# Ranks inside each expert by differences on the matrix engine, and products that nobody reads in its pauses

## The chip, the cores and the metric

The kernel runs on one core of a Trainium2 chip. The metric is the device time of one execution in microseconds (us), lower is better. About 0.2%, or 3.2 us here, is what a measurement of this kernel can tell from no change.

A core has five engines that each work through their own queue in order: TensorE (PE, with its weight loads shown as PEld), VectorE (DVE), ScalarE (ACT), GpSimd (POOL) and SyncE (SP, which only issues DMAs here). They wait for each other by semaphores. TensorE's clock is granted by the chip; the profile gives the share of full speed as PEclk.

## The reference, cut to what matters

Four layers follow each other over 2048 tokens of 256 channels, each a conditioning block and a feed-forward block added to `x`. The change lies in the last feed-forward block, where each of 16 experts takes the 160 tokens with the highest top-1 probability among those that chose it:

```python
    def _L3_ffn_ref(x, Wg, W1, b1, W2, b2):      # n = 16, bt = 2048
        cap = math.ceil(CAP_FACTOR * bt / n)     # 160
        logits = jnp.einsum('btd,dn->btn', x, Wg)
        probs = jax.nn.softmax(logits, axis=-1)
        top1_val = probs.max(axis=-1).reshape(bt)
        top1_idx = probs.argmax(axis=-1).reshape(bt)
        masked = jnp.where(top1_idx[None, :] == jnp.arange(n)[:, None], top1_val[None, :], -jnp.inf)
        vals, idx = jax.lax.top_k(masked, cap)
        valid = jnp.isfinite(vals)
        xe = x_flat[idx]
        h = jax.nn.gelu(jnp.einsum('ncd,ndh->nch', xe, W1) + b1[:, None, :])
        out = jnp.einsum('nch,nhd->ncd', h, W2) + b2[:, None, :]
        safe_idx = jnp.where(valid, idx, bt)
        y_flat = x_flat.at[safe_idx.reshape(-1)].set(out.reshape(-1, d), mode='drop')
```

## The kernel before, in words

**Where the change sits.** `Last` is the last feed-forward block. The 2048 tokens are 16 tiles `t` of 128 and four chunks `q` of 512. A token's place in its expert's list is its rank: how many tokens of the same expert have a higher probability (or the same and an earlier index). `Last.chunk(q)` makes a list of small steps for each chunk, and `Last.finish` runs them in an order written out by hand (`todo`), between the last additions of the conditioning block (`c.pair`, two tiles at a time, whose inputs `yt` come by DMA). The compiler's scheduler then sets the order within each engine.

**The steps of a chunk.** `logits` multiplies by the gate (PE, `l3f_pt`) and copies (ACT, `l3f_lt`). `top` transposes (PE, `l3f_pl`) and finds on DVE the chosen expert `f` and the top probability `val`, with one exponential on ACT. `rows` makes the one-hot `oh` and its running count `cum`, and spreads `f` and `val` of 512 tokens over all 128 partitions: eight PE transposes (`l3f_rb`) and two ACT copies into `HT` (`self.eb`, `self.vb`). `last` is `rows` followed by `keep`, which stores the residual. Then come `beats(t)`, one unit for each tile `t` up to the chunk's own last: 4, 8, 12 and 16 units for chunks 0 to 3, 40 in all.

**A unit before the change.** ACT squares four times the difference of the experts' numbers (`l3f_dq`). DVE compares the probabilities of 512 tokens (fewer on the diagonal) with those of the tile's 128, and asks that the comparison exceed `dq`, which is zero only for the same expert (`l3f_b`, L1822, with the row sums accumulated into `self.acc`). The 16 diagonal units need three more DVE instructions over 128x128 for ties (`l3f_tie`, L1813, L1816, L1817). PE sums `l3f_b` over its partitions with products one column wide (`l3f_cs`, L1829), and DVE subtracts those sums (L1836).

**After the units.** DVE adds up `self.acc` to `l3f_rank` (L1875) and compares the ranks with a row of numbers, half of the tiles at a time (`l3f_A`, L1879); 32 small products (`l3f_pi`, L1884) turn this into token lists, four more (`l3f_pj`, L1892) rearrange the tail, `numbers` makes indices of them, POOL gathers the tokens' rows by indirect DMA (L332), and `Last.run` works through 20 slots: transposes (`ps_cm`, L354), a product (`l3f_ph`, L1945, or `l3f_gh` for a group of four experts), GELU on ACT, a product (`l3f_po`), two additions on DVE, and an indirect DMA to the output (L1933).

PSUM is used through pools: tag `mm` has four buffers, `o` and `t` two each.

Of the kernel before, what the change touches and what calls it, by code (L numbers as in the profile page):

```python
# [86 lines left out]
def _consts(k):  # L87
    nc, cp = k.nc, k.cp
    k.ident = cp.tile([P, P], F32, name="ident")
    make_identity(nc, k.ident)  # L90
    k.ones = cp.tile([P, P], F32, name="ones")
    nc.vector.memset(k.ones, 1.0)

    k.before = cp.tile([P, P], F32, name="before")
    nc.gpsimd.affine_select(out=k.before, in_=k.ones, compare_op=ALU.is_ge, fill=0.0,
                            base=-1, pattern=[[1, P]], channel_multiplier=-1)
    k.after = cp.tile([P, P], F32, name="after")
    nc.gpsimd.affine_select(out=k.after, in_=k.ones, compare_op=ALU.is_ge, fill=0.0,
                            base=-1, pattern=[[-1, P]], channel_multiplier=1)

    k.hm = cp.tile([P, 8], F32, name="hm")
    nc.gpsimd.affine_select(out=k.hm, in_=k.ones[:, 0:8], compare_op=ALU.is_ge, fill=0.0,
                            base=0, pattern=[[-16, 8]], channel_multiplier=1)
    nc.gpsimd.affine_select(out=k.hm, in_=k.hm, compare_op=ALU.is_ge, fill=0.0,
                            base=15, pattern=[[16, 8]], channel_multiplier=-1)
    ii = k.zero.bitcast(I32)[:, 0:CAP]
    nc.gpsimd.iota(ii, pattern=[[1, CAP]], base=0, channel_multiplier=0)
    k.iota = cp.tile([P, CAP], F32, name="iota")
    nc.vector.tensor_copy(k.iota, ii)
    nc.vector.memset(k.zero[:, 0:D], 0.0)  # L110
    nc.vector.memset(k.zero[:, D:], NONE)
    it = cp.tile([P, NT], I32, name="it")
    nc.gpsimd.iota(it, pattern=[[P, NT]], base=0, channel_multiplier=1)
    k.tok = cp.tile([P, NT], F32, name="tok")
    nc.vector.tensor_copy(k.tok, it)
    k.tok2 = cp.tile([P, NT], F32, name="tok2")
    nc.vector.tensor_scalar_mul(k.tok2, k.tok, 2.0)
    k.one16 = cp.tile([P, 1], BF16, name="one16")
    nc.vector.memset(k.one16, 1.0)

    k.small = {}
    for n, c, f in (("L2_wr", 4, 8), ("L2_gw", 2, 8), ("L3_wr", 4, 8), ("L3_Wg", 2, 16)):
        t = k.small[n] = cp.tile([P, c, 32], F32, name="w_" + n)
        nc.gpsimd.memset(t, 0.0)
        nc.scalar.dma_start(t[:, :, 0:f], k.A[n].rearrange("(c p) f -> p c f", p=P))
    for n in ("L2_rb", "L3_rb"):
        t = k.small[n] = cp.tile([P, 8], F32, name="w_" + n)
        nc.scalar.dma_start(t, k.A[n].to_broadcast([P, 8]))
    t = k.small["L3_b1"] = cp.tile([P, 64], F32, name="w_b1")
    nc.scalar.dma_start(t, k.A["L3_b1"])  # L130

    k.cT = cp.tile([P, 2, 2], F32, name="cT")
    nc.sync.dma_start(k.cT, k.A["condT"].rearrange("(c p) b -> p c b", p=P))
# [216 lines left out]
def _channel_major(k, psum, rows):  # L350

    ps = psum.tile([P, 2, P], F32, name="ps_cm", tag="t", bufs=2)
    for c in range(2):
        k.nc.tensor.transpose(ps[:, c, :], rows[:, c * P:(c + 1) * P], k.ident)  # L354
    return ps
# [849 lines left out]

def _shared(k, pool, psum, X, tb, W1, W3, W2, nf, hook=None, mid=None):
# [30 lines left out]
def _back(k, psum, src, dst, t, ref=None):  # L1237
# [6 lines left out]
    k.nc.scalar.copy(dst[:, :, t * P:(t + 1) * P], ps)  # L1244

# [45 lines left out]
class Tokens:  # L1291
# [28 lines left out]
    def back(self, t, ref=None):  # L1320
        _back(self.k, self.psum, self.dst, self.dstT, t, ref)
        self.put = t + 1

# [11 lines left out]
    def pair(self):  # L1335
# [3 lines left out]
        for t in range(self.put, self.added):  # L1339
            self.back(t)  # L1340
# [337 lines left out]
class Last:  # L1678

    E, F = 16, 512

    def __init__(self, k):
# [8 lines left out]
        self.neg = rp.tile([P, NT], F32, name="l3f_neg")  # L1693
        self.cum = rp.tile([P, NT + 1, E], F32, name="l3f_cum")

        self.acc = rp.tile([P, NT, 10], F32, name="l3f_acc")
# [4 lines left out]

        self.vb, self.eb = k.HT[:, 0, :], k.HT[:, 1, :]
# [12 lines left out]
    def begin(self):  # L1715

        k, nc = self.k, self.k.nc
        nc.vector.memset(self.acc, 0.0)
        nc.vector.memset(self.cum[:, 0, :], 0.0)
# [3 lines left out]
        self.weights()  # L1723

# [4 lines left out]
    def chunk(self, q):  # L1729
# [41 lines left out]
        def rows(mul, mm):  # L1771
            nc.vector.tensor_scalar_mul(self.neg[:, ts], got["f"], -4.0)
            oh = self.oh[:, ts, :]
            nc.vector.tensor_tensor(oh, _bc(self.down, 1, [P, 4, E]), _bc(got["f"], 2, [P, 4, E]),
                                    ALU.is_equal)
            for t in range(4 * q, 4 * q + 4):
                nc.vector.tensor_add(self.cum[:, t + 1, :], self.cum[:, t, :], self.oh[:, t, :])
            for src, dst in ((got["f"], self.eb), (self.val[:, ts], self.vb)):
                ps = psum.tile([P, 4, P], F32, name="l3f_rb", tag="mm")
                for j in range(4):  # L1780
                    i = nc.tensor.transpose(ps[:, j, :], src[:, j:j + 1].to_broadcast([P, P]), k.ident)  # L1781
                    behind(i, mm)
                nc.scalar.copy(dst[:, cols], ps.rearrange("p j q -> p (j q)"))
            ps = psum.tile([P, 4, E], F32, name="l3f_pn", tag="mm")
            i = nc.tensor.matmul(ps.rearrange("p t e -> p (t e)"), k.ones,
                                 self.cum[:, ts, :].rearrange("p t e -> p (t e)"), start=True, stop=True)
            behind(i, mm)

            w = pool.tile([P, 4, E], F32, name="l3f_w")
            nc.vector.tensor_mul(w, ps, oh)  # L1790
# [4 lines left out]
        def beats(t):  # L1795

            def unit(mul, mm):
                lo = max(t * P, q * TB)
                own = t >= 4 * q
                dq = pool.tile([P, TB], F32, name="l3f_dq", tag="fa")  # L1800
                n = (q + 1) * TB - lo
                i = nc.scalar.activation(dq[:, 0:n], self.eb[:, lo:lo + n], AF.Square,  # L1802
                                         bias=self.neg[:, t:t + 1], scale=4.0)
                v1 = self.val[:, t:t + 1]

                first = t % 4 == 0
                if first:
                    got["cs"] = psum.tile([P, 4], F32, name="l3f_cs", tag="t", bufs=2)
                a = lo
                if own:  # L1810
                    a = lo + P
                    tie = pool.tile([P, P], F32, name="l3f_tie", tag="xsT", bufs=3)
                    i = nc.vector.scalar_tensor_tensor(tie, self.vb[:, lo:a], v1, k.after, ALU.is_equal,  # L1813
                                                       ALU.mult)
                    behind(i, mul)
                    i = nc.vector.scalar_tensor_tensor(tie, self.vb[:, lo:a], v1, tie, ALU.is_gt, ALU.add)  # L1816
                    i = nc.vector.scalar_tensor_tensor(tie, tie, 1.0, dq[:, 0:P], ALU.mult, ALU.is_gt,  # L1817
                                                       accum_out=self.acc[:, t, 4:5])
                n = (q + 1) * TB - a
                if n:  # L1820
                    w = pool.tile([P, TB], BF16, name="l3f_b", tag="xs", bufs=4)
                    i = nc.vector.scalar_tensor_tensor(w[:, 0:n], self.vb[:, a:a + n], v1,  # L1822
                                                       dq[:, a - lo:a - lo + n], ALU.is_gt, ALU.is_gt,
                                                       accum_out=self.acc[:, t, q:q + 1])
                    behind(i, mul)

                    for j in range(n // P):
                        m = (a + j * P) // P - 4 * q
                        nc.tensor.matmul(got["cs"][:, m:m + 1], w[:, j * P:(j + 1) * P], k.one16,  # L1829
                                         start=first, stop=t % 4 == (2 if own else 3),  # L1830
                                         skip_group_check=True)
                        first = False
                if t % 4 == 3:

                    lo = 1 if own else 0
                    nc.vector.tensor_scalar_mul(self.acc[:, 4 * q + lo:4 * q + 4, 6 + t // 4],  # L1836
                                                got["cs"][:, lo:4], -1.0)
# [14 lines left out]
    def finish(self, c):  # L1852
# [3 lines left out]
        for e in range(E):  # L1856
# [4 lines left out]
                p1[3:7], p3[0:1], p1[7:], p2[2:3], p3[1:2], p2[3:7], p3[2:3], p2[7:], p3[3:]]  # L1861
        for x in todo:
            if callable(x):
                x()
            else:
                for p in x:
                    p(None, None)
# [7 lines left out]
        nc.vector.tensor_reduce(rank, self.acc, AX.X, ALU.add)  # L1875
        ps = k.psum.tile([P, 2, 2, E], F32, name="l3f_pi", tag="t", bufs=2)
        for h in range(2):
# [3 lines left out]
            for j in range(8):  # L1881
                t = 8 * h + j
                for o, r in ((ps[:, 0], slice(0, P)), (ps[0:32, 1], slice(P, CAP))):
                    nc.tensor.matmul(o, A[:, j, r], self.ids[:, t], start=t == 0 and r.start == 0,  # L1884
                                     stop=t == NT - 1, skip_group_check=True)
# [5 lines left out]
        for g in range(4):  # L1891
            nc.tensor.matmul(pg[32 * g:32 * g + 32], k.ident[0:32, 0:32], more[:, :, g::4], start=True,  # L1892
                             stop=True, skip_group_check=True)
# [20 lines left out]
    def run(self):  # L1914
# [70 lines left out]
        for n, i in enumerate(order):  # L1985
            xT = pool.tile([P, 2, P], F32, name="xsT", bufs=3)
            nc.vector.tensor_copy(xT, _channel_major(k, psum, at[i]))
# [154 lines left out]
```

## Time and profile before

| | us |
|---|---|
| median of 3 runs | 1601.93 (1601.33 to 1602.55) |
| the profiled execution, its own time | 1612.81 |
| its span in the profile | 1611.1 |
| mean granted clock of TensorE | 0.953 |

The profiled execution took 10.9 us more than the median of the plain runs. Times in the profile count from the start of its span. The ranks are made between about 1449 and 1508 us of it, the slots of the last block between 1514 and 1600 us. A row of a group shows the line, the engine, what is written and read, the count, the busy time and the mean length of one, and then how long the engine stood idle just before and what released it.

### The profile page before, as it was taken

How to read it: one execution, taken by the hardware profiler on the slowest of the kernel's cores; microseconds unless marked ns; L12 is line 12 of the kernel's file. 1: busy time of each engine (PE TensorE's matmuls, PEld its weight loads, DVE VectorE, ACT ScalarE, POOL GpSimd, SP SyncE). 2: the span in 40 equal slices, each digit the busy share in tenths (PEclk: the TensorE clock that was granted, in tenths of full speed). 3: DMA queues.
4: the chain of work that ended last, by engine and by line, in shares of the span. 5: the costliest groups of instructions: out<-in, count | busy, mean ns of one | idle time of the engine just before them, and what ended most of it. 6: DMA issues, size and time to landing. Idle time of an engine off the chain costs nothing. (4 is left out here: it accounts for less than half of the span.)

```text
span 1611.1 us, 23661 instructions
## 1 busy us (share of the span) xinstructions
PE 1466.1 (91%) x8570; PEld 1021.6 (63%) x8570; DVE 491.7 (31%) x1654; ACT 313.1 (19%) x637; POOL 293.5 (18%) x306
## 2 busy tenths in 40 slices
PE   5879998967999989999999999999999989995697
PEld 2543333533555776555599999999985448863575
DVE  3732221323411344341111111111114414459432
ACT  2312221112111212111111111111112212126322
POOL 0400000300231332023100000000000243430242
PEclk9879999977999999999999999999999999995699
DMA  9759994813211465051143255055517437573271
GB/s 241 262 181 334 343 345 161 246 54 118 83 50 40 148 210 178 27 194 49 40 172 104 101 184 169 30 181 178 175 32 259 149 118 243 186 224 124 59 242 35
DMA packets 184241, 252.46 MB, mean 157 GB/s; under 512 B 17111, under 2 KB 137823, under 8 KB 184112
## 3 DMA queue, kind: packets, MB, share of 16 engines
q1 hardware_dynamic: 164448, 210.92, 40.8%
q0 software_dynamic: 14176, 36.63, 6.4%
q10 hardware_dynamic: 5488, 3.25, 0.7%
q8 instruction: 74, 1.21, 0.3%
q14 instruction: 55, 0.45, 0.1%
HBM read 284.86 MB, written 50.76 MB: 208 GB/s over the span
## 5 line engine op out<-in xcount | busy, mean ns | idle before, releaser
L1229 PE MATMUL spo<-ring,sa 128*128 128x256 f32 x768 | 193.0, 394 | 20.9 <-DVE sa L1226 15.7
L277 POOL DMA_INDIRECT tbuf<-ys,sdst x114 | 112.2, 984 | 539.1 <-ACT ys L1432 228.4
L1229 PEld LDWEIGHTS spo<-ring,sa 128*128 128x128 f32 x768 | 140.6, 192 | 103.0 <-DVE sa L1226 71.9
L1226 DVE TENSOR_TENSOR sa<-ssg,spu 128x512 f32<-128x512 f32 x96 | 65.9, 686 | 331.6 <-PE spu L1219 284.8
L1423 PE MATMUL fpg<-xsT,ring 128*128 128x128 f32 x1152 | 141.6, 276 | 5.9 <-ACT ys L1432 5.9
L1423 PEld LDWEIGHTS fpg<-xsT,ring 128*128 128x128 f32 x1152 | 135.8, 192 | 10.4 <-ACT ys L1432 9.4
L1423 PE MATMUL fpu<-xsT,ring 128*128 128x128 f32 x1152 | 140.4, 275 | 0.0
L1423 PEld LDWEIGHTS fpu<-xsT,ring 128*128 128x128 f32 x1152 | 134.4, 192 | 0.0
L1427 DVE TENSOR_TENSOR fa<-fsg,fpu 128x512 f32<-128x512 f32 x72 | 49.5, 687 | 277.6 <-PE fpu L1423 277.6
L1430 PE MATMUL fpo<-ring,fa 128*128 128x256 f32 x576 | 130.3, 379 | 0.0
L1224 ACT ACTIVATE ssg<-spg 128x512 f32<-128x512 f32 x96 | 57.3, 597 | 349.3 <-PE spg L1219 273.1
L1430 PEld LDWEIGHTS fpo<-ring,fa 128*128 128x128 f32 x576 | 106.7, 190 | 13.0
L1219 PE MATMUL spg<-HT,ring 128*128 128x512 f32 x192 | 100.1, 609 | 5.2 <-PEq L478 2.9
L1219 PE MATMUL spg<-XT,ring 128*128 128x512 f32 x192 | 99.6, 608 | 4.7 <-ACT XT L896 4.7
L1406 PE MATMUL cpo<-ring,ch 128*128 128x256 f32 x312 | 86.8, 401 | 5.0 <-ACT ch L1403 3.5
L1219 PE MATMUL spu<-HT,ring 128*128 128x512 f32 x192 | 90.9, 594 | 0.0
L1219 PE MATMUL spu<-XT,ring 128*128 128x512 f32 x192 | 90.4, 593 | 0.0
L1400 PEld LDWEIGHTS cph<-xsT,ring 128*128 128x128 f32 x624 | 81.8, 191 | 5.0 <-ACT ch L1403 1.1
L1400 PE MATMUL cph<-xsT,ring 128*128 128x128 f32 x624 | 82.4, 275 | 0.7 <-ACT ch L1403 0.7
L1373 DVE COPY xsT<-ps_cm 128x256 f32<-128x256 f32 x138 | 56.8, 421 | 84.0 <-PE ps_cm L354 77.8
L1426 ACT ACTIVATE fsg<-fpg 128x512 f32<-128x512 f32 x72 | 43.0, 597 | 179.6 <-PE fpg L1423 179.6
L1406 PEld LDWEIGHTS cpo<-ring,ch 128*128 128x128 f32 x312 | 53.1, 189 | 19.5 <-ACT ch L1403 12.9
(550 smaller groups left out, 1606.0 us busy)
## 6 DMA issues: line engine op xcount, KB each, us to landing
ring<-in_L_w SPq DMA_DIRECT2D x108, 1024.0 KB
ring<-in_L_r SPq DMA_DIRECT2D x96, 512.0 KB
ring<-in_L_r SPq DMA_DIRECT2D x156, 256.0 KB
xs<-xbuf SPq DMA_DIRECT2D x138, 129.0 KB
ring<-in_L_W SPq DMA_DIRECT2D x32, 512.0 KB
yt<-tbuf SPq DMA_DIRECT2D x48, 256.0 KB
xbuf<-ACC SPq DMA_DIRECT2D x1, 6063.0 KB
ring<-in_L_s SPq DMA_DIRECT2D x6, 512.0 KB
```

What stands on the lines that cost most here:

```text
L277: i = k.nc.gpsimd.indirect_dma_start(out=self.ap, out_offset=bass.IndirectOffsetOnAxis(ap=idx, axis=0), in_=rows, in_offset=None, **end)
L1219: mm = nc.tensor.matmul(ps, W[:, c, f * P:(f + 1) * P], X[:, c, cols], start=c == 0, stop=c == 1)
L1224: nc.scalar.activation(sg, pg, AF.Silu)
L1226: mul = nc.vector.tensor_mul(a, sg, pu)
L1229: mm = nc.tensor.matmul(po[g // 2][:, g % 2, :], a[:, g * P:(g + 1) * P], W2[:, f, :], start=f == 0 and g % 2 == 0, stop=f == nf - 1, skip ...
L1373: turned = nc.vector.tensor_copy(xT, _channel_major(k, self.psum, xs))
L1400: nc.tensor.matmul(ph[:, f, :], R1[:, c, f * P:(f + 1) * P], xT[:, c, :], start=c == 0, stop=c == 1)
L1406: nc.tensor.matmul(po, h[:, f, :], R2[:, f, :], start=f == 0, stop=f == 1)
L1423: nc.tensor.matmul(ps[:, j, :], W[:, c, (f0 + j) * P:(f0 + j + 1) * P], xT[:, c, :], start=c == 0, stop=c == 1)
L1426: nc.scalar.activation(sg, pg, AF.Silu)
L1427: nc.vector.tensor_mul(a[:, f0:f0 + 4, :], sg, pu)
L1430: nc.tensor.matmul(po, a[:, f, :], W2[:, f, :], start=f == 0, stop=f == 4 * nh - 1)
```

## The change

The comparison becomes an arithmetic difference that PE makes. For every token a vector of up to 128 channels is built in `self.z`: the one-hot of its expert, the probability cut into three BF16 parts, and constants. With a left and a right form of it (`sides`, stored as BF16 in `HT`), one product over 128 channels gives a number that is positive only where the one token beats the other and both have the same expert. On the diagonal a second, 128-wide product with `k.not16` decides the ties. A unit is now: one product (`l3f_d`, plus the small one on the diagonal), a sign with row sums, on DVE for even tiles and on ACT for odd ones, and one product with a matrix of ones that sums over partitions (`l3f_cs`, now as wide as the unit, over all units of the chunk in one PSUM buffer). At the end of a chunk ACT copies one row of it (`l3f_less`), four tiny products turn it (`l3f_pc`) and DVE copies it. The ACT units count in signs of -1 and +1, which constants in `self.acc` correct; the rank is halved at the end.

Besides, `_warm` issues products into a PSUM buffer that nothing reads: four after each of the three `c.pair`, six after the last unit, and ten after `l3f_pj`, with the slots' transposes ordered behind those ten. On SP, the last store of token rows to `hx` and two stores of `out` change places. `begin` gains nine small memsets on DVE and 16 on POOL, and the constants gain two small DVE instructions.

```diff
+def _warm(k, psum, ref, n):
+    ps = psum.tile([P, TB], F32, name="warm", tag="mm")
+    for _ in range(n):
+        i = k.nc.tensor.matmul(ps.rearrange("p (j q) -> p j q", q=P), k.ident16, _bc(k.ident16, 1, [P, 4, P]),
+                               start=True, stop=True, skip_group_check=True)
+        _behind(k, i, ref)
+        ref = i
+    return ref
...
         def rows(mul, mm):
-            nc.vector.tensor_scalar_mul(self.neg[:, ts], got["f"], -4.0)
-            oh = self.oh[:, ts, :]
+            oh, z, v, n = self.oh[:, ts, :], self.z, self.val[:, ts], self.PARTS
...
+            nc.vector.tensor_copy(z[:, :, :, 0:E], _bc(oh, 2, [P, 4, 2, E]))
+            r = pool.tile([P, 4], F32, name="l3f_r")
+            for i in range(3):
+                to = zf[:, :, n + 2 * i + 1:n + 2 * i + self.K + 1:self.K - 1]
+                nc.vector.tensor_copy(to, _bc(v if i == 0 else r, 2, [P, 4, 2]))
+                if i < 2:
+                    nc.vector.tensor_tensor(r, v if i == 0 else r, to[:, :, 0], ALU.subtract)
+            for side, to in enumerate(self.sides(q)):
+                ps = psum.tile([P, 4, P], F32, name="l3f_ps", tag="mm")
+                for j in range(4):
+                    i = nc.tensor.matmul(ps[0:self.K, j, :], z[:, j, side, :], k.ident16, start=True,
+                                         stop=True, skip_group_check=True)
+                    behind(i, mm)
+                nc.scalar.copy(to, ps[0:self.K].rearrange("k j p -> k (j p)"))
...
-            for src, dst in ((got["f"], self.eb), (self.val[:, ts], self.vb)):
-                ps = psum.tile([P, 4, P], F32, name="l3f_rb", tag="mm")
-                for j in range(4):
-                    i = nc.tensor.transpose(ps[:, j, :], src[:, j:j + 1].to_broadcast([P, P]), k.ident)
-                    behind(i, mm)
-                nc.scalar.copy(dst[:, cols], ps.rearrange("p j q -> p (j q)"))
...
-                i = nc.scalar.activation(dq[:, 0:n], self.eb[:, lo:lo + n], AF.Square,
-                                         bias=self.neg[:, t:t + 1], scale=4.0)
...
+                d = psum.tile([P, TB], F32, name="l3f_d", tag="mm")
+                left, right = self.sides(t // 4)[0], self.sides(q)[1]
+                i = nc.tensor.matmul(d[:, 0:n], left[:, (t % 4) * P:(t % 4 + 1) * P], right[:, TB - n:TB],
+                                     start=True, stop=not own, skip_group_check=True)
                 if own:
-                    tie = pool.tile([P, P], F32, name="l3f_tie", tag="xsT", bufs=3)
-                    i = nc.vector.scalar_tensor_tensor(tie, self.vb[:, lo:a], v1, k.after, ALU.is_equal,
-                                                       ALU.mult)
...
+                    nc.tensor.matmul(d[:, 0:P], k.ident16, k.not16, start=False, stop=True,
+                                     skip_group_check=True)
+                w = pool.tile([P, TB], BF16, name="l3f_b", tag="xs", bufs=4)
+                to = self.acc[:, t, q:q + 1]
+                if self.on_act(t):                     # t % 2 == 1
+                    nc.scalar.activation(w[:, 0:n], d[:, 0:n], AF.Sign, bias=k.minus, scale=2.0 ** 30,
+                                         accum_out=to)
+                else:
+                    i = nc.vector.scalar_tensor_tensor(w[:, 0:n], d[:, 0:n], 0.0,
+                                                       k.two.to_broadcast([P, n]), ALU.is_gt, ALU.mult,
+                                                       accum_out=to)
...
-                    for j in range(n // P):
-                        m = (a + j * P) // P - 4 * q
-                        nc.tensor.matmul(got["cs"][:, m:m + 1], w[:, j * P:(j + 1) * P], k.one16,
-                                         start=first, stop=t % 4 == (2 if own else 3),
-                                         skip_group_check=True)
...
+                if t == 0:
+                    got["cs"] = psum.tile([P, TB], F32, name="l3f_cs", tag="o", bufs=2)
+                nc.tensor.matmul(got["cs"][:, TB - n:TB], k.one16, w[:, 0:n], start=t == 0,
+                                 stop=t == 4 * q + 3, skip_group_check=True)
+                if t == 4 * q + 3:
+                    less = pool.tile([1, TB], F32, name="l3f_less", tag="fa")
+                    nc.scalar.activation(less, got["cs"][0:1, :], AF.Copy, scale=-1.0)
+                    ps = psum.tile([P, 4], F32, name="l3f_pc", tag="t", bufs=2)
+                    for j in range(4):
+                        i = nc.tensor.matmul(ps[:, j:j + 1], less[:, j * P:(j + 1) * P], k.ones[0:1, 0:1],
+                                         start=True, stop=True, skip_group_check=True)
+                    nc.vector.tensor_copy(self.acc[:, ts, 6], ps)
+                    return i
...
         for x in todo:
             if callable(x):
-                x()
+                _warm(k, k.psum, x(), 4)
             else:
                 for p in x:
-                    p(None, None)
+                    ref = p(None, None) or ref
+        ref = _warm(k, k.psum, ref, 6)
...
+        nc.vector.tensor_scalar_mul(rank, rank, 0.5)
...
+        self.ref = _warm(k, k.psum, ref, 10)
...
-            nc.vector.tensor_copy(xT, _channel_major(k, psum, at[i]))
+            nc.vector.tensor_copy(xT, _channel_major(k, psum, at[i], self.ref))
```

## The prediction, made before the changed kernel ran

> **What bounds the kernel now.** I read the page's slices first, for the place of the change on the time axis, then busy time by stretch, the chain of waits, and the groups by shape.
>
> ```profile
> span 1611.1 us, 23661 instructions
> ...
> PEclk9879999977999999999999999999999999995699
> ```
>
> A slice is 40.3 us. The clock of PE falls to 5 and 6 tenths only in the slices where the ranks are made (1450 to 1530). Busy time by stretch (length, then PE, PEld, DVE, ACT, POOL, clock, DMA share, GB/s):
>
> ```profile
> 1449.70:1480.80 31.10, 18.24 (x152) 13.24 (x152) 27.87 (x135) 18.45 (x41) 2.35 (x1) 0.61 0.47 163
> 1480.80:1500.70 19.90, 5.19 (x73) 3.47 (x72) 19.08 (x81) 15.29 (x24) 0.00 (x0) 0.50 0.00 1
> 1500.70:1508.80 8.10, 4.83 (x40) 3.52 (x40) 4.67 (x17) 0.11 (x1) 0.00 (x0) 0.50 0.00 0
> 1508.80:1513.90 5.10, 0.66 (x2) 0.30 (x3) 0.74 (x4) 0.00 (x0) 3.84 (x5) 0.50 0.49 122
> 1513.90:1518.00 4.10, 4.08 (x20) 4.10 (x20) 0.00 (x0) 0.18 (x1) 1.90 (x2) 0.51 0.70 224
> 1518.00:1600.00 82.00, 80.25 (x604) 61.32 (x603) 26.12 (x61) 21.95 (x69) 32.06 (x33) 1.00 0.44 145
> ```
>
> From 1480.8, when chunk 3's spread copies are in, DVE is saturated: 19.08 of 19.90 us, ACT 15.29, PE 5.19. The slots after 1518 are PE's at full clock, and their products are untouched. The chain of waits (start, length, what) says that nothing runs beside the way from the ranks to the slots:
>
> ```profile
> 1480.23 0.59 ACT HT L1783
> ...
> 1500.68 0.33 DVE l3f_rank L1875
> 1501.03 1.50 DVE l3f_A L1879
> 1502.58 4.56 PE l3f_pi L1884 x32
> ...
> 1510.14 3.65 DMA ACC<-hx,l3f_src
> ...
> 1514.37 3.41 PE l3f_ph L1945 x16
> ```
>
> A microsecond taken out between 1480 and 1508 should come out at the end: the DMA share is 0.00 there, so no weights are still on their way that could be late instead. The groups of 1480.8 to 1500.7 show what DVE does:
>
> ```profile
> L1802 ACT ACTIVATE l3f_dq<-HT,l3f_neg 128x512 f32<-128x512 f32 x16 | 11.1, 721 | 2.1 <-DVE l3f_b L1822 1.4 <-DVE l3f_tie L1817 0.7
> L1822 DVE SCALAR_TENSOR_TENSOR l3f_b<-HT,l3f_val,l3f_dq 128x512 bf16<-128x512 f32 x14 | 10.1, 748 | 0.5 <-ACT l3f_dq L1802 0.4
> ...
> L1813 DVE SCALAR_TENSOR_TENSOR l3f_tie<-HT,l3f_val,after 128x128 f32<-128x128 f32 x8 | 2.8, 348 | 0.0
> L1816 DVE SCALAR_TENSOR_TENSOR l3f_tie<-HT,l3f_val,l3f_tie 128x128 f32<-128x128 f32 x8 | 2.8, 346 | 0.0
> ```
>
> A wide `l3f_b` occupies DVE 0.67 us from start to start (accumulator read included; its mean of 748 ns overlaps the next), one of 256 elements 0.41, a diagonal's three tie steps 0.74 together.
>
> **The change, part by part.** Twenty units run after chunk 3's sides are in, before and after.
>
> *The final stretch.* PE gets a product `l3f_d` and a product `l3f_cs` for each unit: 28 of 512 columns, 4 of 384, 4 of 256, 12 of 128 (eight of these twice the diagonal's), 18,432 columns. No row shows a BF16 product of 512 columns. Two rows bound it. From above, an FP32 record of 512 columns: L1219, 100.1 us for 192, 0.52 us at full clock. From below, a BF16 weight load:
>
> ```profile
> L1884 PEld LDWEIGHTS <-l3f_A 128*128 128x128 bf16 x16 | 1.7, 104 | 3.4 <-DVE l3f_A L1879 2.9
> ```
>
> 104 ns for 128 columns at clock 0.50 is 0.42 us for 512, so 0.21 at full clock. By the first, 36 products' worth takes 18.7 us and the gain is gone; by the second 7.8 us at full clock and 15.4 at half. I take the second: same type, same columns through the array. DVE keeps nine wide signs at 0.67, two of 256 at 0.41 and three small steps: 7.2 us (a row that reads PSUM, L1649, has 0.69 for its 512; 0.2 either way is 1.8 us, hidden). ACT gets seven wide signs, two of 384, two narrow, two `l3f_less`. No row has a sign with sums; the nearest, L770, takes 722 ns and 186 ns for the accumulator, 0.81 from start to end: 7 x 0.81 + 2 x 0.68 + 2 x 0.45 + 2 x 0.6 = 9.1 us (7.6 with the 0.60 of a copy from PSUM, 9.8 with 0.91). So DVE's 19.9 becomes PE's 7.8 to 15.4 beside ACT's 9.1: the clock decides.
>
> *The clock.* Windows of 3.41 us on the grid on which the recorded clock changes:
>
> ```profile
> 1449.67:1453.09 3.42, 2.32 (x28) 1.59 (x28) 2.47 (x15) 1.84 (x6) 0.00 (x0) 1.00 0.99 354
> 1453.09:1456.50 3.41, 1.71 (x24) 1.08 (x24) 3.41 (x15) 2.31 (x8) 0.00 (x0) 1.00 1.06 391
> 1456.50:1459.91 3.41, 1.95 (x9) 1.33 (x9) 2.63 (x18) 0.90 (x3) 0.00 (x0) 0.50 0.76 268
> 1466.74:1470.15 3.41, 3.10 (x27) 2.07 (x26) 3.02 (x15) 1.88 (x5) 0.00 (x0) 0.50 0.30 68
> 1514.53:1517.94 3.41, 3.41 (x18) 3.41 (x17) 0.00 (x0) 0.12 (x1) 1.26 (x2) 0.50 0.71 220
> ```
>
> The clock was lost after a window that was half busy, its longest pause 1.2 us (1.7 in the one before). A window 91% busy did not bring it back, a full one did. The Trainium skill, page "TensorE: Matmul & The Clock Gate", Part 1, says otherwise of the loss: the clock halves after a whole idle window of about 3.4 us. By that rule no pause of the new stage is long enough, the clock stays, and the sum is 1586.6 (below). By the row it falls where PE is half busy, as it will be between the pairs: each group of four unread products adds only 0.9 us to a window of 1.7. The row decides; I expect a stage of mixed clock. The same page (Part 4) says that PE's transposes do not count as busy in the usual way. That would explain the 91%, since 2.0 of the 3.10 us were transposes (`l3f_rb`). By it the new stretch, plain products only, regains the clock in its first well-filled window (the stretch then 11.3); by the row alone 91% is too little and the stretch stays half (17.9). I take one and a half windows, 5.1 us, at half clock.
>
> Length then: 5.1 us do 33% of 15.4; the rest is 67% of 7.8, 5.2; a start of 0.3 and a tail of 1.9 (last sign 0.81, its `l3f_cs` 0.22, `l3f_less` 0.4, four `l3f_pc` 0.3, copy 0.2): 12.5 instead of 19.8, **-7.3**. With full clock ACT's 9.1 and the ends make 10.7.
>
> *Before it, the way to chunk 3's sides.* DVE loses half of twenty units' comparisons (some 10 x 0.54) and eight diagonals' ties (8 x 0.74), 11 us of its 27.9, and gains about five serial steps of 0.2 in each chunk's `rows` (three copies into `z`, two subtractions), 4 us. But chunk 3's chain starts only with the last pair's additions, at 1461.2 in the trace, which wait for their DMA. From there it goes through PE's queue five times (transposes back, `l3f_pt`, `l3f_pl`, two sides), now behind two wide products for each unit and four unread ones (0.9 us, 1.7 at half clock); DVE's `top` and `rows` wait behind those. Laid out in the new queue order with the durations above, the sides are ready at 1477.4 with full clock, 1479.7 mixed and 1485.0 at half, where the trace has 1480.8. Taken: **-0.8** (-3.4 to +4.2). `keep` and the exchanged stores on SP cost nothing: the chain has no piece on SP, and `hx` is written long before the gather.
>
> *Ranks to gather.* The halving is one DVE step more on the chain, +0.2. The six unread products end within the 2.0 us that `l3f_rank` and `l3f_A` take (1.3 us at full clock; 2.6 at half would hold up `l3f_pi` by 0.6). `l3f_pi` takes 4.56 us at half clock; half of it at full clock is -0.9. Together **-0.7** (-1.4 to +0.8).
>
> *The slots' start.* The ten unread products behind `l3f_pj` take 4.3 us at half clock, and the gather 1.1 + 5 us: the slots' transposes, ordered behind them, wait for the gather anyway. If the clock is up, the first `l3f_ph` costs 1.8 us instead of 3.41; half of that, **-0.8** (0 to -1.7).
>
> *Elsewhere.* Two small DVE steps stand before the first reciprocals at 14 us: **+0.3**. The memsets of `begin` (391 us) fall into DVE's pauses of about 4 us between `sa` steps: 0.
>
> Sum: -0.8 - 7.3 - 0.7 - 0.8 + 0.3 = -9.3. For the profiled execution, 1612.81 (span 1611.1, 1.7 around it), that is 1603.5; it ran 10.9 above the median of the plain runs, 1601.93, and none of that lies in these steps, so 1592.6.
>
> **The rivals.** *The clock stays granted* (0.20): -3.4 - 9.1 - 1.4 - 1.7 + 0.3 = -15.3, 1586.6. For it: the unread products fill pauses, and DVE makes fewer of them. Against: the half-busy row.
>
> *PE becomes the bound* (0.11), the slower side. The clock falls at the pairs as before and stays at half. The sides come at 1485.0, PE needs 15.4 us for the units, and with its in-order waits for the four `mm` buffers the last write into `l3f_acc` comes at 1505.8 against 1500.7: +5.1, +0.2, +0.3, 1607.5. It decides where PE's mean clock in the stage is below about 0.63 (on the line from -15.3 at 1.0 to +5.6 at 0.5). For it: 0.50 held from 1456.5 to 1517.9, through a window of 91%. Against: at half clock PE has hardly a pause, and that brings the clock back.
>
> *Gained in the stretch, lost before it* (0.09): the unread products do not hold the clock, and it returns only late. Sides at 1484, +3.2; stretch 15.5, -4.3; ranks and slots -0.4; start +0.3: -1.2, 1600.7.
>
> **How the numbers follow.** The mixed clock has 0.60, and its time is the forecast, 1592.6. A difference under 0.2%, 3.2 us, can't be told from none. The first two cases are faster, 0.80; the lost gain is within, 0.09; PE's bound is slower, 0.11. The range leaves out the slower case and the far end of the full clock: 1584.5 to 1601.
>
> **What would show it.** Right: clock above 0.63 between 1450 and 1515; about 12.5 us from the second `l3f_ps` copy of chunk 3 to the last write of `l3f_acc`, with PE busy nine tenths of it and DVE under 8 us; records of `l3f_d` in stretches of 0.22 and of 0.43; ACT's signs near 0.81; the first `l3f_ph` at 1.8. Wrong: sides later than 1483; a clock of 0.5 throughout (PE is the bound); signs over 0.95 on ACT (ACT is); slots after 1518 of another length than 82.0 us.

## Result and profile after

| | before | changed |
|---|---|---|
| median of 20 runs | 1600.36 us (1595.14 to 1605.51) | 1596.21 us (1590.25 to 1600.59) |
| ratio, 95% interval | | 0.9973 (0.9961 to 0.9985) |
| profiled execution, its own time | 1612.81 us | 1599.90 us |
| its span | 1611.1 us | 1597.8 us |

The ratio is a gain of 4.3 us (2.4 to 6.2) where 9.3 were forecast; 1596.21 lies in the range. The two profiled executions differ by 12.9 us, which is not the change alone: the last `sa` multiplication of the conditioning block, ahead of nearly all of the change, starts at 1444.19 us before and at 1437.85 after. From here on, times are counted from that start ("after `sa`"), which takes the drift out:

| after `sa`, us | before | changed | changed, again |
|---|---|---|---|
| chunk 3's sides in `HT` (copies end) | 36.6 | 37.7 | 37.5 |
| `l3f_rank` starts | 56.5 | 51.7 | 52.9 |
| first `l3f_ph` starts | 70.0 | 64.5 | 66.2 |
| end | 166.9 | 159.9 | 161.6 |

The last column is a second profile of the changed kernel, from the experiments. So the part after `sa` is 7.0 and 5.3 us shorter. The kernel before has one profile only; the kernel with the unread products alone (below), which makes its ranks as before, has 56.2 at `l3f_rank` and 165.6 at the end, so a microsecond of either difference may be scatter. The page of the changed kernel, span and clock:

```profile
span 1597.8 us, 23714 instructions
...
PEclk9989999987999999999999999999999999998999
```

The 5 and 6 of the rank slices have become 8 and 9. Busy time by stretch, columns as in the prediction:

```profile
1443.40:1475.50 32.10, 25.37 (x180) 14.85 (x182) 20.59 (x108) 14.13 (x39) 2.35 (x1) 0.84 0.42 144
1475.50:1489.50 14.00, 12.83 (x71) 6.72 (x71) 7.87 (x27) 10.22 (x28) 0.00 (x0) 1.00 0.01 2
1489.50:1497.30 7.80, 6.15 (x49) 3.85 (x47) 4.87 (x18) 0.00 (x0) 0.02 (x1) 0.86 0.00 0
1497.30:1502.10 4.80, 4.05 (x11) 1.32 (x9) 0.77 (x4) 0.00 (x0) 3.83 (x4) 0.52 0.46 125
1502.10:1506.30 4.20, 3.79 (x31) 3.58 (x32) 0.76 (x2) 1.14 (x4) 1.89 (x2) 1.00 0.71 213
1506.30:1588.30 82.00, 80.02 (x599) 61.23 (x598) 25.37 (x59) 21.96 (x68) 32.89 (x33) 1.00 0.43 146
```

The second row is the final stretch: 14.0 us, DVE down from 19.08 to 7.87, ACT 10.22, and PE, 5.19 before, now 12.83 of 14.00 at full clock. PE is now the longest in place of DVE; whether it also sets the stretch is tested below. The groups of that stretch:

```profile
L1870 DVE SCALAR_TENSOR_TENSOR l3f_b<-l3f_d,two 128x512 bf16<-128x512 f32 x10 | 6.8, 690 | 2.5 <-PE l3f_d L1857 1.6 <-PE l3f_d L1861 0.9
L1877 PE MATMUL l3f_cs<-l3f_b,one 128*128 128x512 bf16 x18 | 6.0, 378 | 0.2
L1867 ACT ACTIVATE l3f_b<-l3f_d,minus 128x512 bf16<-128x512 f32 x8 | 5.4, 680 | 2.1 <-PE l3f_pc L1884 0.9 <-PE l3f_d L1857 0.7 <-PE l3f_cs L1877 0.4
L1857 PE MATMUL l3f_d<-HT 128*128 128x512 bf16 x15 | 4.8, 379 | 0.2 <-issue 0.2
L1867 ACT ACTIVATION_READ_ACCUMULATOR l3f_b<-l3f_d,minus 128x1 f32 x12 | 2.3, 194 | 0.0
...
L1884 PE MATMUL l3f_pc<-ones,l3f_less 1*128 1x1 f32 x16 | 2.1, 248 | 0.7 <-ACT l3f_less L1881 0.7
...
L1870 DVE DVE_READ_ACCUMULATOR l3f_b<-l3f_d,two 128x1 f32 x12 | 1.0, 83 | 0.0
```

Each sign has one accumulator read, twelve on ACT and twelve on DVE: 24 units fall into this stretch, chunk 3's sixteen and eight of chunk 2. DVE and ACT, the bound before, now idle before their signs and are released by PE; one of ACT's waits ends with `l3f_pc`. A record of 378 ns overlaps the next: from start to start a wide product takes 0.216 us. Four `l3f_pc` products, one column each, take eight records and 1.05 us. The chain of waits shows them twice:

```profile
1480.57 1.31 PE l3f_pc L1884 x8
...
1481.97 0.79 ACT l3f_b L1867 x2
...
1486.90 0.58 PE l3f_cs L1877 x3
...
1487.50 0.59 ACT l3f_less L1881
...
1488.14 1.06 PE l3f_pc L1884 x8
...
1489.53 0.28 DVE l3f_rank L1927
```

At 1480.57 the turning of chunk 2's sums stands in PE's queue in front of chunk 3's products; at the end chunk 3's own is a tail that nothing covers: 2.0 us from the end of the last `l3f_cs` to `l3f_rank`.

### The profile page after: what moved, and what is told of

Same layout as the page of the kernel before. It is cut to its first block, busy times and chain, and to the rows that moved or that the text cites. A ratio compares the mean times of both kernels' runs of the same rounds, so it can differ in the third digit from the quotient of the medians.

```text
span 1597.8 us, 23714 instructions
## 1 busy us (share of the span) xinstructions
PE 1484.7 (93%) x8611; PEld 1025.8 (64%) x8614; DVE 474.9 (30%) x1586; ACT 303.4 (19%) x641; POOL 294.0 (18%) x321
## 5 line engine op out<-in xcount | busy, mean ns | idle before, releaser
L1394 DVE COPY xsT<-ps_cm 128x256 f32<-128x256 f32 x138 | 56.8, 422 | 85.8 <-PE ps_cm L360 85.4
L1427 PEld LDWEIGHTS cpo<-ring,ch 128*128 128x128 f32 x312 | 53.2, 189 | 21.0 <-ACT ch L1424 15.4
```

Source lines behind the costliest of these rows:

```text
L1394: turned = nc.vector.tensor_copy(xT, _channel_major(k, self.psum, xs))
L1427: nc.tensor.matmul(po, h[:, f, :], R2[:, f, :], start=f == 0, stop=f == 1)
```

## The experiments

Ratios are to the kernel before, on the same chip; "rank" is the start of `l3f_rank` after `sa` in the profile, "stretch" the time from chunk 3's sides to it.

| kernel | ratio (95%) | sides | rank | stretch | end after `sa` |
|---|---|---|---|---|---|
| changed, first | 0.9973 (0.9961 to 0.9985) | 37.7 | 51.7 | 14.0 | 159.9 |
| changed, again | 0.9962 (0.9948 to 0.9975) | 37.5 | 52.9 | 15.4 | 161.6 |
| no unread products | 0.9962 (0.9948 to 0.9976) | 38.0 | 52.0 | 14.0 | 162.0 |
| unread products alone | 1.0001 (0.9987 to 1.0015) | 36.2 | 56.2 | 20.0 | 165.6 |
| all signs on DVE | 1.0011 (1.0002 to 1.0021) | 42.8 | 59.4 | 16.6 | 167.6 |
| sums by columns | 0.9916 (0.9898 to 0.9934) | 36.2 | 46.5 | 10.2 | 154.4 |
| no four | 0.9963 (0.9952 to 0.9973) | 38.1 | 52.3 | 14.1 | 162.1 |
| early order | 0.9985 (0.9973 to 0.9998) | 34.7 | 54.4 | 19.7 | 162.3 |
| early order, sums by columns | 0.9916 (0.9904 to 0.9929) | 33.8 | 46.8 | 13.0 | 155.1 |
| late turning | 0.9966 (0.9953 to 0.9980) | 37.6 | 51.4 | 13.8 | 160.9 |
| one part | 0.9964 (0.9947 to 0.9982) | 36.3 | 50.5 | 14.2 | 160.2 |
| sums by columns, chunk 1 first | 0.9925 (0.9904 to 0.9946) | 36.7 | 47.3 | 10.6 | 157.2 |
| every `l3f_d` twice | 0.9991 (0.9980 to 1.0002) | 37.7 | 56.8 | 19.1 | 166.1 |

**Do the unread products hold the clock?** Without all of them:

```diff
-                _warm(k, k.psum, x(), 4)
+                x()
...
-        ref = _warm(k, k.psum, ref, 6)
...
-        self.ref = _warm(k, k.psum, ref, 10)
+        self.ref = ref
```

> The changed kernel without its unread products (none after the pairs, none after the last unit, none after l3f_pj). Theory A, the unread products hold or bring back the clock: without them the clock is 0.5 through most of 1440 to 1500, the stretch from chunk 3's sides to the last l3f_acc grows from 13.9 us to 17 or more, the first l3f_ph takes 3.4 us instead of 1.8, and the time is 3 to 8 us above the changed kernel's, about that of the kernel before (ratio 0.999 to 1.003). Rival B, the wide l3f_d and l3f_cs products fill PE enough by themselves: clock near 1.0 in the stretch, only the first l3f_ph slow (+1.6) and 1 to 3 us of products gone from PE's queue, ratio 0.996 to 0.998.

Ratio 0.9962, the second measurement of the changed kernel to the digit; the stretch is 14.0 us, its clock 1.00 (the first row below). Theory A is wrong and B holds. In this run the clock came back at 1463.9 (the second row), after a window busy for 3.20 of 3.42 us, mostly with wide `l3f_d` and `l3f_cs` products:

```profile
1474.70:1488.60 13.90, 12.45 (x69) 6.50 (x68) 7.81 (x27) 10.19 (x27) 0.00 (x0) 1.00 0.01 2
...
1460.48:1463.90 3.42, 3.20 (x10) 1.15 (x10) 3.03 (x18) 1.93 (x6) 0.00 (x0) 0.50 0.28 69
```

The first sixteen `l3f_ph` took 3.2 us instead of 1.95.

> The kernel before with the unread products alone, at the same places (four after each pair, six after the last unit, ten after l3f_pj); ranks are made as before. Theory A: DVE still sets the 19.8 us stretch, so only l3f_pi (up to 2.2 us less) and the first l3f_ph (1.6 us less) gain, ratio 0.998 to 1.000. Rival, the unread products make all of the changed kernel's gain: ratio 0.997 or less. Rival, they stand in the way: above 1.000.

In the kernel before they change nothing that can be told: 1.0001, stretch 20.0 us, DVE still full and PE idle at half clock:

```profile
1470.20:1490.20 20.00, 6.12 (x76) 3.87 (x76) 18.89 (x79) 15.28 (x24) 0.00 (x0) 0.50 0.01 1
```

So the gain is not theirs. The groups of four alone (`x()` in place of `_warm(k, k.psum, x(), 4)`), beside the changed kernel on the same chip:

> The changed kernel without the four unread products after each pair (the six and the ten stay). In the run without any, l3f_rank came 52.05 us after the last sa, with them 51.7. Theory (they do nothing between the pairs; the wide products hold the clock): rank at 51 to 52.5, ratio equal to that of the changed kernel within 0.001. Rival (they pay): rank 2 us or more later, ratio 0.001 to 0.002 above the changed kernel's. Rival (they cost their own 0.9 to 1.7 us on chunk 3's chain): as much below it.

> The changed kernel once more, on the same chip as the three below, so that they can be compared with it. Ratio 0.996 to 0.9985. Measured in the profile from the last sa multiplication of the conditioning block on (1444.19 before, 1437.85 after), where the work before it no longer counts, the kernel before takes 56.5 us to l3f_rank and 166.9 us to the end, the changed kernel 51.7 and 160.0; if the profiled execution was typical, 51 to 53 and 159 to 161 come again, and if it was a lucky one (a gain of 4 us is what the medians show), 162 to 163.

0.9963 and 0.9962: nothing to be told apart. The second profile of the changed kernel had its clock at 0.92 in the stretch instead of 1.00, which goes with its 15.4 us and 161.6 (15.4 at a mean of 0.92 would be 14.2 at full clock, if PE sets it). The ten behind `l3f_pj` may do something, but no run leaves out them alone: of the twelve profiles of kernels with them (the changed kernel twice) nine have the first sixteen `l3f_ph` at 1.95 us and three near 3.5; of the two without, one has 3.6 and one 3.2. That is at most 1.7 us, about 0.1%, which no ratio here resolves.

**Which engine?** With `on_act` returning False:

> The changed kernel with all 20 signs of the last stretch on DVE and none on ACT (the constants follow). If PE's order and the turning of the sums set the stretch (theory A), DVE's 14 x 0.69 + 2 x 0.6 + 2 x 0.42 + 2 x 0.3 = 12.3 us just about fits beside PE, and the stretch grows by 1 to 2 us over 13.9: ratio 0.9975 to 0.9985. If the split between the two engines is what made the gain (rival), the stretch goes to 17 or more and the ratio to 1.000.

```profile
1472.20:1488.80 16.60, 14.67 (x72) 6.94 (x72) 13.46 (x51) 2.50 (x4) 0.00 (x0) 1.00 0.01 1
```

The stretch grew by 2.5 us over the first profile of the changed kernel, somewhat more than the theory's 1 to 2. The ratio, 1.0011, is the rival's: no gain is left. Chunk 3's sides came 5 us later, because more signs on DVE stand in front of the chains of small steps there: behind chunk 2's `top`, seven of them occupy DVE from 29.1 to 32.6 us after `sa`, where the changed kernel has one. The expectation counted the last stretch alone; giving half of the signs to ACT is worth 6.5 to 7.7 us up to `l3f_rank`.

**Is it the turning of the sums?** Sums by columns, as before the change:

```diff
-                nc.tensor.matmul(got["cs"][:, TB - n:TB], k.one16, w[:, 0:n], start=t == 0,
-                                 stop=t == 4 * q + 3, skip_group_check=True)
+                for j in range(n // P):
+                    m = 4 - n // P + j
+                    i = nc.tensor.matmul(got["cs"][:, m:m + 1], w[:, j * P:(j + 1) * P], k.one16[:, 0:1],
+                                         start=t == 0 and j == 0, stop=t == 4 * q + m,
+                                         skip_group_check=True)
                 if t == 4 * q + 3:
...
+                    nc.vector.tensor_scalar_mul(self.acc[:, ts, 6], got["cs"][:, 0:4], -1.0)
                     return i
```

> The changed kernel with the column sums made as before the change: the signs as weights against one column of ones, one product for each 128 tokens, added over the chunk in four columns, so that l3f_less and the four l3f_pc products fall away (DVE negates the four columns). Theory A, the turning is what the forecast mis-sized (l3f_pc takes 1.05 us for 0.3, and blocks PE's queue while ACT copies): the end of chunk 3 loses 1.5 us and the end of chunk 2 1.2 us, stretch 11 to 12, ratio 0.995 to 0.996. Rival, four weight loads and short products for each unit cost PE as much as they save (4 x 0.11 against 0.22 for 20 units, 4 us): stretch 14 or more, ratio 0.997 or above.

More than expected: 0.9916, 13.5 us under the kernel before (1604.54 on that chip). The stretch is 10.2 us, and the three engines are close together (PE, PEld, DVE, ACT, POOL as above):

```profile
1471.80:1482.00 10.20, 9.94 (x119) 5.56 (x119) 8.10 (x28) 8.40 (x25) 0.00 (x0) 0.89 0.01 2
```

Its group of sums by columns:

```profile
L1879 PE MATMUL l3f_cs<-one,l3f_b 128*128 128x1 bf16 x84 | 5.4, 166 | 0.2
```

84 records, yet they start only 25 ns apart: four of them (512 tokens) hold PE for 0.11 us, where the wide `l3f_cs` holds it for 0.216. The rival had priced each of them at 0.11, the length of a weight-load record. So the wide form costs PE twice over: about 2 us in 24 units, and twice 1.05 us of turning with the wait for `l3f_less`.

Does the turning cost where it stands, or as work? Chunk 2's turning moved into chunk 3's units (`turn()` holds the `l3f_less` and `l3f_pc` lines unchanged):

```diff
+                if q == 3 and t == 7:
+                    self.late()
                 if t == 4 * q + 3:
...
-                    return i
+                    return turn() if q != 2 else i
...
+            if q == 2:
+                self.late = turn
```

> The changed kernel with the turning of chunk 2's sums (l3f_less, l3f_pc, the copy) moved behind chunk 3's eighth unit; everything else as changed. In the changed kernel PE waits for l3f_less at 1480.0 and then works 1.05 us on l3f_pc, with DVE idle 0.88 and ACT 0.91 beside it. Theory A (the blocked queue is one of two parts of what the turning costs, the other being 1.6 us at the end and the rest the width of l3f_cs): the stretch from the sides to l3f_rank loses 0.5 to 1.2 us of its 14.0 to 15.4, ratio 0.9955 to 0.9965. Rival (the block drains all three engines and is most of the 4 to 5 us between the changed kernel and the one with sums by columns): stretch 11 to 12, ratio 0.994. Rival (turning in the middle is hidden): no difference.

Stretch 13.8 instead of 14.0, ratio 0.9966: no gain that can be told, which is closest to the last of the three expectations. The eight records now stand at 1486.46 and hold PE for 1.0 us there. Either the turning costs PE's time wherever it is put, which fits a stretch that PE sets, or it is hidden in both places; this run does not tell the two apart. The direct test doubles PE's work alone:

```diff
+                nc.tensor.matmul(d[:, 0:n], left[:, (t % 4) * P:(t % 4 + 1) * P], right[:, TB - n:TB],
+                                 start=True, stop=True, skip_group_check=True)
                 i = nc.tensor.matmul(d[:, 0:n], left[:, (t % 4) * P:(t % 4 + 1) * P], right[:, TB - n:TB],
```

> The changed kernel with every l3f_d product issued twice into the same place, the second overwriting the first: 0.22 us more of PE at full clock for each wide unit, 17 to 18 such in the last stretch (4 of 384, 256 and 128 columns among the 20 pairs), 3.6 us in all, and nothing more on DVE or ACT. Theory (PE and its order set the stretch; late_turn showed that the turning costs the same 1.05 us wherever it stands): the stretch from chunk 3's sides to l3f_rank grows from 14.0 to 15.4 by 3 to 4 us, ratio 0.9985 to 1.000. Rival (the signs on DVE and ACT set it and PE only waits for them): it grows by less than 1.5 us, ratio 0.9965 to 0.9975.

The stretch is 19.1 us, 5.1 more than the first profile of the changed kernel at nearly the same clock (0.99 against 1.00), and 3.7 more than the second, for 4.3 us of added products (the trace has 10,240 columns of them in the stretch, at 0.216 us for 512). Groups of that stretch:

```profile
L1872 DVE SCALAR_TENSOR_TENSOR l3f_b<-l3f_d,two 128x512 bf16<-128x512 f32 x10 | 6.9, 692 | 5.8 <-PE l3f_d L1859 3.8 <-PE l3f_d L1863 2.0
...
L1869 ACT ACTIVATE l3f_b<-l3f_d,minus 128x512 bf16<-128x512 f32 x8 | 5.5, 687 | 6.0 <-PE l3f_d L1859 6.0
```

DVE's and ACT's busy times are those of the changed kernel; their idle time before the wide signs, of which 2.5 and 0.7 us were waits for `l3f_d`, grew to 5.8 and 6.0 us, all for `l3f_d`. That PE's queue sets the stretch of the changed kernel is shown: what is added to PE comes out about in full, where the rival had less than 1.5 us. That queue also waits for signs, so their time counts too, as the run with all signs on DVE showed.

**Why are chunk 3's sides later than before?** Two theories, one run for each. One BF16 part of the probability instead of three (`range(1)`, and no subtraction):

> The changed kernel with the probability in one BF16 part instead of three; the two subtractions and two copies of each chunk's rows are left out, and with them the low bits of the probability, so that near values compare as equal. It prices the serial steps. Theory A (they stand on the chain of each chunk, one chunk behind the other): chunk 3's sides come 37.5 us after the last sa in the changed kernel, and 0.8 us for each of the chunks in series less here: 34.5 to 36.5, ratio 0.9945 to 0.9955. Rival B (the order is what makes them late: all eight additions of the last two pairs stand ahead of chunk 1's top on DVE, whose sides come at 24.8 instead of 17.4): sides 36.8 or later, ratio 0.996 to 0.997.

Sides 1.1 to 1.3 us sooner than in the two profiles of the changed kernel, rank 1.2 to 2.4. The sides, at 36.3, lie at the late end of A's 34.5 to 36.5; the ratio, 0.9964, is B's but does not resolve it. The two parts left out cost 0.3 us for each chunk, not 0.8, and that is about what separates the changed kernel's sides from those before. The order:

```diff
-        todo = [c.pair, p0[0:2], p1[0:1], c.pair, p1[1:2], p0[2:4], c.pair, p2[0:1], p0[4:], p1[2:3], p2[1:2],
-                p1[3:7], p3[0:1], p1[7:], p2[2:3], p3[1:2], p2[3:7], p3[2:3], p2[7:], p3[3:]]
+        todo = [c.pair, p0[0:2], p1[0:2], c.pair, p1[2:3], p0[2:4], c.pair, p2[0:1], p0[4:], p1[3:5], p2[1:2],
+                p1[5:7], p3[0:1], p1[7:], p2[2:3], p3[1:2], p2[3:7], p3[2:3], p2[7:], p3[3:]]
```

> The kernel with the sums by columns, and chunk 1's top moved ahead of the second pair in the hand-written list, its rows behind that pair, two of its units ahead of chunk 2's top. If rival B of one_part holds (the order makes the sides late), chunk 1's sides come 16 to 19 us after the last sa instead of 22.3, chunk 3's at 34 to 35 instead of 36.2, l3f_rank at 44 to 45.5 instead of 46.5, ratio 0.990 to 0.991. If the last pair's transfers and the chain behind them set chunk 3's sides alone, chunk 1 comes sooner and chunk 3 does not: rank 46 to 47, ratio 0.9915.

Chunk 1's sides came at 20.2 instead of 22.3, but the last pair's additions ended 3.4 us later (19.4 after `sa`), and chunk 3's sides at 36.7 instead of 36.2. Chunk 1 sooner does not make chunk 3 sooner, as the second expectation had it (rank 47.3 and ratio 0.9925 lie a little above its 46 to 47 and 0.9915). Its reason is not shown: the last pair's additions came 3.4 us later and the sides only 0.5, so that pair alone does not set them either, and what does stays open. A list with chunk 3's steps pulled forward:

```diff
+        todo = [c.pair, p0[0:2], p1[0:1], c.pair, p1[1:2], p0[2:4], c.pair, p2[0:1], p3[0:1], p0[4:], p1[2:3],
+                p2[1:2], p2[2:3], p3[1:2], p1[3:7], p3[2:3], p1[7:], p2[3:], p3[3:]]
```

> The changed kernel with another order of the hand-written list: the gate products of chunk 3 stand right behind those of chunk 2, its top ahead of chunk 1's units after the first, its rows ahead of most units, so that chunk 3's sides are ready sooner. Theory: in the changed kernel chunk 3's l3f_pl stood 4.3 us in PE's queue behind units and the turning of chunk 1's sums, which is why its sides came 37.6 us after the last sa instead of sooner; now they come at 30 to 33, the stretch behind them is longer (more units left, 17 to 18 us), and l3f_rank comes 2 to 3 us sooner: ratio 0.995 to 0.9965. Rival: the units bind, whatever the order; rank as before, ratio 0.997. Rival: without units beside it the chain leaves engines idle, and it comes later: above 0.998.

> The same order together with the column sums made as before the change (cols, ratio 0.9916, l3f_rank 46.5 us after the last sa). Theory: the two gains add, rank at 43 to 45, ratio 0.989 to 0.9905. Rival: with the turning gone the units bind and the order is worth nothing: rank at 46 to 47, ratio 0.9915.

The sides did come sooner, at 34.7 and 33.8, and all of that came back as a longer stretch, with more units left for it (19.7 and 13.0): rank 54.4 in the first, later than the changed kernel's, and 46.8 in the second, about that of the column sums alone. In neither did sooner sides make the ranks sooner. The version to keep is the one with sums by columns in the list's own order.

## Why the prediction held, and where it was off

| step, us | forecast | profile | profile again |
|---|---|---|---|
| chunk 3's sides | -0.8 | +1.0 | +0.9 |
| final stretch | -7.3 | -5.8 | -4.5 |
| ranks to first `l3f_ph` | -0.7 | -0.6 | -0.2 |
| first sixteen `l3f_ph` | -0.8 | -1.7 | -1.7 |
| rest of the slots | 0 | +0.1 | +0.1 |
| sum after `sa` | -9.6 | -7.0 | -5.3 |

**What bounds: right.** DVE's 19.9 us went, PE became the longest, and what was taken out there arrived at the end: the slots from 1506.3 on show PE at 80.02 of 82.0, as before. The start's +0.3 lies below what these runs resolve. That 1596.21 lies in the range says little by itself: the range ends at 1601, above the 1600.36 of the kernel before, and the forecast gain of 9.3 us lies outside the measured interval of 2.4 to 6.2.

**The final stretch: right about PE, mis-sized in PE's sum.** The clock was granted throughout in the first profile (1.00). For that case the rival "the clock stays granted" had 10.7 us, of ACT's 9.1 and the ends; it took 14.0, and the doubled `l3f_d` shows PE's queue, not ACT, to be what sets it. The price of a product was good: 0.216 us for 512 columns at full clock, 0.43 at half in the column kernel, against 0.21 and 0.42. The reason behind it was weaker than it looked: the weight load that it was scaled from is a record of 97 ns at full clock and of 104 at half, not twice as long.

What failed is the rest of the sum. "Twenty units" was a miscount: the rows of the kernel before show 14 wide `l3f_b` and 8 diagonals, 22 units, in that stretch, and 24 run there after the change. Nine and seven wide signs, as the prediction has them for DVE and ACT, fit 22 units; PE's columns were counted for twenty. The trace has 20,480 columns there, 8.6 us, instead of 18,432 and 7.8 (0.21 times 36 would be 7.6), and three of the 28 wide `l3f_d` of all chunks have no record, so it may be a little more. The tail gave 0.3 us to four `l3f_pc`; they take 1.05, and the same turning for chunk 2 falls inside this stretch and was not counted: 2.1 us. And PE's queue, in order, alternates between products that wait for a sign and products that feed one: at most 3.3 us of the 14.0 remain for waits and ends, where the sum had 1.9. So PE's sum at full clock, 10.0 us, was short by 0.8 of products, 1.8 of turning and 1.4 of waits. That 14.0 came within 1.5 us of the forecast 12.5 is in part luck: the clock, expected at half for 5.1 us, hid some of this by not falling. ACT's sign with its accumulator read took 0.79 against 0.81, DVE's 0.69 against 0.67.

**Ranks to the first `l3f_ph`: near, by luck.** The sum let half of `l3f_pi` run at full clock for -0.9 us, as if it took half the time there. In the traces the 32 products start 0.121 us apart at full clock and 0.140 at half.

**Chunk 3's sides: wrong sign, small.** +1.0 where -0.8 was forecast (its own 1479.7 against 1480.8 would be -1.1), inside the -3.4 to +4.2 given. Two of the three parts of the probability account for about 1.2 us, by the run with one part; how much of the rest PE's queue took is not shown.

**The clock: the row was the better guide to the loss, but the unread products mattered less than the prediction thought.** In the changed kernel, on the grid of the recorded clock:

```profile
1440.50:1443.91 3.41, 1.56 (x10) 0.82 (x8) 3.34 (x9) 2.97 (x7) 2.35 (x1) 1.00 1.02 296
1447.32:1450.74 3.42, 3.42 (x16) 1.57 (x18) 0.91 (x3) 0.78 (x3) 0.00 (x0) 0.50 0.92 328
1454.15:1457.56 3.41, 2.23 (x18) 1.59 (x16) 3.27 (x9) 1.35 (x5) 2.35 (x1) 1.00 0.62 218
1457.56:1460.98 3.42, 2.99 (x21) 1.48 (x22) 1.78 (x16) 0.69 (x2) 0.00 (x0) 0.50 0.86 280
1491.70:1495.11 3.41, 3.41 (x30) 2.65 (x29) 1.23 (x1) 0.00 (x0) 0.00 (x0) 1.00 0.00 0
1498.52:1501.94 3.42, 2.83 (x8) 0.89 (x6) 0.42 (x1) 0.00 (x0) 2.75 (x3) 0.50 0.62 167
```

It was lost after the first and third of these windows, 46% and 65% busy. The first held hardly anything but FP32 transposes, so if those do not count it was nearly idle; the third was two thirds full of records, mostly plain products, and there the rule of a whole idle window does not describe this case, as the prediction held. It came back after the second and fourth, both of which hold four unread products; but the kernel without them got it back from `l3f_d` and `l3f_cs`. The prediction gave "PE becomes the bound at half clock" 0.11; PE did become the bound, at full clock, and at that the kernel is still faster.

## What to carry to other kernels

When work moves to an engine that was idle, count the units from the trace's rows, and add up every small product that comes with them, and each place where the engine's queue waits in order, before trusting the sum of the wide ones: here four one-column FP32 products cost as much as five wide BF16 products, with a row copy ahead of them and nothing to cover the last set. Sums over partitions came cheaper here with the data as weights and one column of ones than with a matrix of ones (0.11 us against 0.216 for 512 tokens, and nothing to turn afterwards). If profiles drift by several microseconds, measure from a landmark just ahead of the change, and double the suspected engine's work to see whether it is the bound.

## What the runs showed of the hardware

A window recorded as fully busy can still lose the clock: 1491.70 to 1495.11 in the rows above holds nothing but `l3f_pi` products of 32 columns, one every 0.12 us and recorded as 3.41 of 3.41 us busy, and the clock stood at half from 1495.11 on. The window from 1498.52, 2.83 of 3.42 busy with the wide unread products, brought it back, while one of 3.10 of 3.41, mostly FP32 transposes, had not done so in the kernel before. So the recorded busy share alone does not decide it. These three windows would fit a count of columns streamed by plain products, but no run isolates that, and it stays open.
